# Two layers of a graph transformer on one core: VectorE and GpSimd in program order, a third tile's own query, queries moved ahead in layer 1, weight loads moved to GpSimd

## The chip, the core and the metric

The kernel runs on one core of a Trainium2 chip. A core has engines that run side by side, each with its own stream of instructions: TensorE (PE) multiplies matrices into an accumulation memory (PSUM), VectorE (DVE) and ScalarE (ACT) work elementwise, GpSimd (POOL) does small elementwise work and starts gathers and scatters by index, SyncE (SP) starts transfers. Each engine takes its instructions in the order in which they stand in its stream, and waits at an instruction until what it reads is there and what it overwrites is free. The metric is the device time of one execution in microseconds; the time before is the median of three runs, 1954.13 us (1949.94 to 1956.24).

## What is computed

The reference, cut to what matters. There are 2708 tokens of width 512 and a symmetric adjacency matrix with about eight neighbours a token. Both layers are the same, with their own weights.

```python
def layer(h, adj, Wq, bq, Wk, bk, Wv, bv, Wo, bo, W1, b1, W2, b2, g1, s1, g2, s2):
    n = h.shape[0]                                   # 2708
    mask = adj.astype(float32) + eye(n)
    q = (h @ Wq.T + bq).reshape(n, 8, 64)            # 8 heads of 64
    k = (h @ Wk.T + bk).reshape(n, 8, 64)
    v = (h @ Wv.T + bv).reshape(n, 8, 64)
    scores = einsum('nhd,mhd->hnm', q, k) / sqrt(64)
    scores = where(mask == 0, -1e9, scores)
    ctx = einsum('hnm,mhd->nhd', softmax(scores), v).reshape(n, 512)
    h1 = layer_norm(h + ctx @ Wo.T + bo, g1, s1)
    ff = relu(h1 @ W1.T + b1) @ W2.T + b2            # 512 -> 2048 -> 512
    return layer_norm(h1 + ff, g2, s2)
out = layer(layer(x, adj, *weights0), adj, *weights1)
```

## The kernel before, in words

The tokens make 22 tiles of 128 (the last has 20). Attention is done by edges: a token has at most 22 neighbours, so instead of full scores the kernel makes a list of neighbours for each token, sorts the tokens by the number of their neighbours, and gathers for each slot of a list one row of 1024 numbers (key and value) per token. Tile g of the sorted order has `CAPS[g]` slots, from 22 to 3. A second path, `by_rows`, computes the same without lists; it runs behind a flag that is set where a list does not fit, and it does not run here.

Stages of the first path, `by_edges`:

1. *Keys* (`first`). For each of 22 tiles, TensorE makes k and v from x and the weights Wk, Wv (`project`, eight instructions of 128x512 each). VectorE adds the bias to k (L910), ScalarE copies v (L912), and a transfer writes both to memory. Beside it `lists(t)` reads 128 rows of the adjacency (1.35 MB), adds the diagonal on GpSimd (L683), turns them into codes on ScalarE (L687), and finds the neighbours with MAX8 on VectorE (11 instructions of L690, then three MAX8 and two MATCH_REPLACE). With `LEAD = 1.3` the code writes 1.3 lists a tile. At tile `QT = 6` the bias row bq is made from a column (`turned_row`): four products with the identity on VectorE (`dg`, L559), four matmuls (`pr<-dg`, L565), a copy (L566). Wo and the first two weight pairs W1, W2 are loaded near the end of the stage, by SyncE.
2. *Queries of layer 0* (`first_queries`). TensorE makes the queries of 22 tiles, VectorE scales them (L947), and they go to memory (q_d). In between the lists are ranked and inverted (`ranked`, `inverted`, L843 and L852), which gives `ident_i`, the token in each place of the sorted order. Everything that goes by the sorted order is gathered by GpSimd with it. The first two tiles of the order get their query here from their own gathered rows (`own_rows`, `own_query`), at query `OWN = 6`, so that their attention can begin before all queries are in memory.
3. *Feed-forward of layer 0* with attention beside it. Blocks are pairs of tiles in the order (20, 19), (18, 17), (7, 9), (6, 10), (5, 11), (0, 16), (1, 15), (2, 14), (3, 13), (4, 12), (21, 8). In a block, `feed_forward` runs 16 steps f: four matmul pairs into `pf` (L1428), relu on ScalarE into `ft` (L1439), and three steps later two accumulations into the block's accumulators a0 and a1 (L1401). During the steps of block k the attention of block k + 1 is brought to its end: at step 10 its context `cx` is turned (`tp<-ident,cx`, L1236), at step 11 it is projected with Wo (L578), added to the residual (L1363) and normed (`norm`, L1217 to L1230, with `rd` on GpSimd, L1226); after step 15 the result h is turned for the next block. At a block's end the accumulators are added to h (L1460) and normed. In layer 0 the next layer's keys and values of the block before follow in steps 5 to 8 (`keys_values`). The rows bk and bq for layer 1 are turned in blocks 1 and 3: `dg` at step 1, `pr` at step 3.
4. *Layer 1* the same way, from its own queries: the queries of the first `AHEAD = 8` blocks stand ahead of its feed-forward, those of the others in blocks 0 to 2. At the end `checked` makes the flag, which the engines load before they branch.

Attention is a generator (`attend`) of chunks of two slots. A chunk's `weights` multiplies the gathered keys by the query (L1100) and sums them to scores (L1106); one chunk later `weigh` takes the exponentials on ScalarE (L1119) and weighs the values on ScalarE (L1126) and VectorE (L1132, added up in L1139); two chunks later, at a tile's last chunk, `sums` closes the tile (L1147, L1151, L1159, and the reciprocal L1162); three chunks later `divided` makes `cx` on ScalarE (L1170). Gathers (L1063) are written three chunks ahead of their use. `advance(more)` adds to a credit and runs chunks until it is used up, a chunk of two slots costing one:

```python
        while credit > 0 and len(got) < CXB - 1:
...
                advance(PACE[n] if k else 0.8 if f < 11 else 0.4)
```

so that `PACE` chunks stand beside each step, and at most two finished tiles wait in `got`.

**What sets the order on each engine.** Within `tc.manual_schedule(engines=...)` the named engines keep the order in which the code writes their instructions. Outside it a planner sorts an engine's instructions by its own estimate of when each can run. TensorE, ScalarE and SyncE are in program order throughout (L495). GpSimd is in program order up to the end of layer 0's first block (L1608, closed at L1703). VectorE is in the planner's order for the keys, in program order from the last two key tiles to step 14 of layer 0's first block (L901, L1610, closed at L1650), and in the opening of layer 1 (L1620). Instructions that are written after such a region may still be put between those inside it.

## Time and profile before

| | us |
|---|---|
| median of three runs | 1954.13 |
| the profiled execution | 1960.03 |
| its span, first to last instruction | 1958.1 |
| TensorE busy | 1856.4 |
| VectorE busy | 1328.4 |
| ScalarE busy | 933.0 |
| GpSimd busy | 804.6 |
| mean granted TensorE clock | 0.979 |

The prediction reads four views: the page (busy time of each engine), the waits (who waited for whom), busy time by stretch, and the timeline of an engine (start, duration, engine, line, operation, output<-inputs, count, and in brackets the idle time before it and what ended it). PE is TensorE, DVE VectorE, ACT ScalarE, POOL GpSimd. In the table by stretch the columns are: from:to, length, busy us of PE, its weight loads, DVE, ACT and POOL with numbers of instructions, then the granted TensorE clock, the busy share of the transfer engines, and GB/s. The keys take the first 160 us, the queries of layer 0 go to 261, layer 0's feed-forward to 1118, layer 1's opening to 1212.

### The profile page before, as it was taken

Reading aid. Unit: us, or ns where it says so; the run is one execution under the profiler, and the core shown is the slowest. Engines: PE = TensorE matmul, PEld = TensorE weight load, DVE = VectorE, ACT = ScalarE, POOL = GpSimd, SP = SyncE. Lnnn points to the kernel's source line nnn. Section 1 sums busy time; section 2 is a strip of 40 time slices with the busy share of each in tenths; the row PEclk is TensorE's granted clock in tenths of the full one; section 3 lists DMA queues with packets and bytes.
Section 4 is the critical chain, followed back from the end, with each engine's and each line's share of the span. In section 5 each row is a group of like instructions: output and inputs, shape, how many; then the busy total and the mean of one; then the engine's idle time right before and its main releaser. Section 6 shows DMA issues by size and latency. Waiting matters only on the chain. (4 is left out here: it accounts for less than half of the span.)

```text
span 1958.1 us, 20848 instructions
## 1 busy us (share of the span) xinstructions
PE 1856.4 (95%) x6160; PEld 1094.8 (56%) x6160; DVE 1328.4 (68%) x2181; ACT 933.0 (48%) x3217; POOL 804.6 (41%) x709
## 2 busy tenths in 40 slices
PE   8998987999999999999999997789899999999996
PEld 4443454655656556566566534456566665666663
DVE  5887676686857868668423256666987998878421
ACT  4561344464545655546422123545475766654520
POOL 2111566453544736545211041333554775546100
PEclk9999998999999999999999999899999999999998
DMA  8988956465645746544210785635664766644000
GB/s 314 344 310 286 348 201 232 160 208 174 219 153 183 244 156 220 181 162 132 102 54 33 263 324 173 208 118 176 215 232 162 245 224 218 197 154 133 17 6 14
DMA packets 133659, 366.91 MB, mean 187 GB/s; under 512 B 19290, under 2 KB 39594, under 8 KB 130828
## 3 DMA queue, kind: packets, MB, share of 16 engines
q0 software_dynamic: 69136, 246.88, 37.9%
q1 hardware_dynamic: 52756, 98.61, 14.6%
q10 hardware_dynamic: 11644, 20.00, 2.8%
q8 instruction: 50, 0.82, 0.2%
q14 instruction: 73, 0.60, 0.1%
HBM read 314.79 MB, written 50.65 MB: 187 GB/s over the span
## 5 line engine op out<-in xcount | busy, mean ns | idle before, releaser
L1063 POOL DMA_INDIRECT kv<-kv_d,listed x420 | 546.6, 1301 | 456.6 <-DVE acc L1139 277.2
L1428 PE MATMUL pf<-hT,w 128*128 128x256 f32 (+1 forms) x2816 | 636.1, 373 | 7.4 <-ACT ft L1439 4.4
L1401 PE MATMUL a<-w,ft 128*128 128x512 f32 x1312 | 618.4, 598 | 11.0 <-DVE h L1460 7.4
L1428 PEld LDWEIGHTS pf<-hT,w 128*128 128x128 f32 x2816 | 520.9, 191 | 182.2 <-issue 103.6
L1100 DVE TENSOR_TENSOR kv<-kv,q 128x1024 f32<-128x1024 f32 (+3 forms) x222 | 255.0, 1159 | 196.6 <-DMA kv<-kv_d,listed 157.9
L1439 ACT ACTIVATE ft<-pf,b 128x256 f32<-128x256 f32 (+1 forms) x336 | 153.9, 463 | 454.3 <-PE pf L1428 454.0
L1401 PEld LDWEIGHTS a<-w,ft 128*128 128x128 f32 x1312 | 248.5, 192 | 203.4 <-issue 168.9
L1126 ACT ACTIVATE kv<-kv,p 128x64 f32<-128x64 f32 x1232 | 311.0, 335 | 5.0
L1106 DVE TENSOR_REDUCE sc<-kv 128x16 f32<-128x1024 f32 (+3 forms) x222 | 254.5, 1154 | 2.0
L1139 DVE TENSOR_TENSOR acc<-acc,kv 128x1024 f32<-128x1024 f32 (+2 forms) x178 | 204.3, 1148 | 20.4 <-ACT kv L1126 17.8
L1226 POOL TENSOR_TENSOR rd<-va,mhalf 128x1 f32<-128x1 f32 (+1 forms) x88 | 90.4, 1027 | 294.9 <-DVE va L1224 294.0
L578 PE MATMUL o<-wo,cT 128*128 128x512 f32 x336 | 149.8, 598 | 0.5 <-ACT cT L1241 0.5
L1132 DVE TENSOR_TENSOR kv<-kv,p 128x512 f32<-128x512 f32 (+1 forms) x178 | 121.8, 685 | 35.0 <-ACT p L1119 35.0
L1119 ACT ACTIVATE p<-sc,listed 128x8 f32<-128x8 f32 x420 | 103.0, 294 | 75.2 <-DVE sc L1106 75.2
L1170 ACT ACTIVATE cx<-acc,su 128x64 f32<-128x64 f32 (+1 forms) x352 | 88.5, 333 | 81.0 <-DVE su L1162 59.8
L578 PEld LDWEIGHTS o<-wo,cT 128*128 128x128 f32 x336 | 64.1, 192 | 82.3 <-issue 72.6
L690 DVE MAX8 tops<-code 128x8 f32<-128x247 f32 (+2 forms) x242 | 83.8, 403 | 23.3 <-ACT code L687 23.2
L687 ACT ACTIVATE code<-aj 128x2708 bf16<-128x2708 int32 (+1 forms) x22 | 73.3, 3331 | 52.6 <-POOL aj L683 52.6
L1230 DVE SCALAR_TENSOR_TENSOR h<-h,rd,ln_b 128x512 f32<-128x512 f32 (+1 forms) x88 | 65.7, 748 | 41.3 <-POOL rd L1226 41.3
L1126 ACT ACTIVATE acc<-kv,p 128x64 f32<-128x64 f32 (+1 forms) x352 | 88.8, 334 | 1.4
L1460 DVE TENSOR_TENSOR h<-a,h 128x512 f32<-128x512 f32 (+1 forms) x44 | 29.9, 680 | 83.3 <-PE a L1401 44.5
L1488 ACT COPY kvs<-v 128x512 f32<-128x512 f32 (+1 forms) x22 | 12.9, 585 | 152.2 <-PE v L578 132.6
(168 smaller groups left out, 1578.6 us busy)
## 6 DMA issues: line engine op xcount, KB each, us to landing
aj<-in_adj SPq DMA_DIRECT2D x21, 1354.0 KB, 8.9
kv_d<-kvs ACTq DMA_DIRECT2D x21, 512.0 KB, 6.5
w<-in_W SPq DMA_DIRECT2D x20, 512.0 KB, 7.5
xg<-in_xT SPq DMA_DIRECT2D x19, 512.0 KB, 9.2
kv<-kv_d,listed POOLq DMA_INDIRECT x420, 5.8
w<-in_W ACTq DMA_DIRECT2D x12, 512.0 KB, 7.6
q_d<-qs SPq DMA_DIRECT2D x22, 256.0 KB, 3.7
zT_d<-zT SPq DMA_DIRECT2D x22, 256.0 KB, 4.8
```

Of the source, the lines that this page charges most:

```text
L578: nc.tensor.matmul(o[:r], xs(c), wm[:, c, :], start=(c == 0), stop=(c == NC - 1))
L1063: return nc.gpsimd.indirect_dma_start(out=to, out_offset=None, in_=table[:, :], in_offset=bass.IndirectOffsetOnAxis(ap=s, axis=0), bounds_ ...
L1100: nc.vector.tensor_tensor(kv[:r, :c, :DM], kv[:r, :c, :DM], self.q[:r].unsqueeze(1).to_broadcast([r, c, DM]), ALU.mult,)
L1106: nc.vector.tensor_reduce(self.sc[:r, s0 : s0 + c, :], kv[:r, :c, :DM].rearrange("p s (h d) -> p s h d", d=DK), AX.X, ALU.add,)
L1119: nc.scalar.activation(p[:r, s, :], self.sc[:r, s, :], AF.Exp, bias=minus[:r, g, s : s + 1])
L1126: nc.scalar.activation(to[:, i, hd], kv[:r, i, DM + h * DK : DM + (h + 1) * DK], AF.Copy, scale=p[:r, s0 + i, h : h + 1],)
L1132: nc.vector.tensor_tensor(to[:, 0, :].rearrange("p (h d) -> p h d", d=DK), kv[:r, 0, DM:].rearrange("p (h d) -> p h d", d=DK), p[:r, s0, : ...
L1139: nc.vector.tensor_tensor(self.acc[:r, :c, :], self.acc[:r, :c, :], kv[:r, :c, DM:], ALU.add)
L1226: nc.gpsimd.tensor_tensor(rd[:r], va[:r], mhalf[:r], ALU.pow)
L1401: nc.tensor.matmul(a[:r], fts[f][:, c0 : c0 + r], self.w2[f // 2][:, f % 2, :], start=(f == 0), stop=(f == NFC - 1),)
L1428: nc.tensor.matmul(pf[:, :w], self.w1[f // 2][:, c, f % 2 * P : f % 2 * P + P], hT[:, c, :w], start=(c == 0), stop=(c == NC - 1),)
L1439: nc.scalar.activation(ft[:, :w], pf[:, :w], AF.Relu, bias=self.b1[:, f : f + 1])
```

## The change

All engines named in `by_hand` now include VectorE and GpSimd, so every engine keeps the order of the code from the first instruction to the last; the regions for single stretches are gone. With it parts of the code are moved:

- A third own query: tile `order[2]` gets its rows with the first two, and its query five tiles after theirs; `OWN` is 7. The lists of the other tiles are all fetched during the queries (`LISTS`), none in block 0. The adds of the last key tile (`last_keys`) stand behind the inversion.
- `AHEAD` is 10: in layer 1, 16 queries stand ahead of block 0's context and four behind it; only block 0 still has queries in its steps.
- Three finished tiles may wait in `got`, `PACE` has three values for a block (steps 0 to 2, 3 to 10, 11 to 15), and in layer 0's first block the turn and projection stand at steps 12 and 13.
- Wo, Wq and four pairs W1, W2 of layer 0 are loaded by GpSimd; the fifth pair by ScalarE.
- Small sums of biases (`unsettled`, `settle`) are made at fixed places.
- The check and the load of its flag move from the end into steps 8 and 14 of the last block.

```diff
-AHEAD = 8
+AHEAD = 10
-OWN = 6
-LISTS = (6, 9, 11, 17, 18, 19)
+OWN = 7
+LISTS = (6, 9, 11, 14, 15, 17, 18, 19, 20, 21)
-PACE = (0.62, 0.72)
+PACE = ((0.45, 0.8, 0.55), (0.5, 0.8, 0.7))
...
         mybir.EngineType.SP,
+        mybir.EngineType.DVE,
+        mybir.EngineType.Pool,
     )
     ctx.enter_context(tc.manual_schedule(engines=set(by_hand)))
...
-            nc.sync.dma_start(out=t[:, c : c + k, :], in_=src[:, c : c + k, :])
+            (by or nc.sync).dma_start(out=t[:, c : c + k, :], in_=src[:, c : c + k, :])
...
-            if t == NT - 2:
-                in_turn.enter_context(tc.manual_schedule(engines={mybir.EngineType.DVE}))
...
             if t == QT:
-                wq = wts.tile([P, NC, DM], F32, tag="wq", name="wq")
-                for c in range(NC):
-                    nc.gpsimd.dma_start(out=wq[:, c, :], in_=chunked(w["Wq"])[:, c, :])
+                wq = matrix(w, "Wq", "wq", nc.gpsimd)
                 turning = turned_row(cols[1], "bq", DK**-0.5)
                 bq = next(turning)
                 finish(turning)
-        in_turn.close()
...
                 evicted(0, held, qs)
-                last_keys()
             if t == 3:
                 inverted(parts)
+                last_keys()
...
-                for g in blocks[0]:
+                for g in order[:3]:
                     own[g] = at.tile([P, DM], F32, tag="q", name="q", bufs=QB)
...
-                xrs = [own_rows(g) for g in blocks[0]]
+                xrs = [own_rows(g) for g in order[:3]]
...
+            if t == OWN + 5:
+                own_query(order[2], zTs[2], to[order[2]], bq, wq)
...
-            self.wo = matrix(w, "Wo", "wo")
+            self.wo = matrix(w, "Wo", "wo", nc.gpsimd if self.n == 0 else None)
...
+        def settle(self):
+            for t in self.unsettled:
+                if isinstance(t, tuple):
+                    nc.vector.tensor_tensor(t[0], t[0], t[1], ALU.add)
+                else:
+                    nc.vector.tensor_scalar(t, t, -1.0, None, ALU.mult)
+            self.unsettled = []
...
+    def settled():
+        held = small.tile([P, 1], F32, tag="held", name="held", bufs=1)
+        nc.vector.tensor_reduce(held, flags, AX.X, ALU.min)
+        pr = ps.tile([P, DM], F32, tag="g", name="pr")
+        nc.tensor.matmul(pr[:1, :1], ones[:, :1], held, start=True, stop=True)
+        nc.vector.tensor_scalar(redo, pr[:1, :1], P - 0.5, None, ALU.is_lt)
+        return nc.values_load(redo[0:1, 0:1], min_val=0, max_val=1)
...
-        while credit > 0 and len(got) < CXB - 1:
+        while credit > 0 and len(got) < CXB:
...
-            now.load_w1(t + 2 - NT)
-            now.load_w2(t + 2 - NT)
+            now.load_w1(t + 2 - NT, nc.gpsimd)
+            now.load_w2(t + 2 - NT, nc.gpsimd)
...
-        if t > 4 and t % 2 and len(now.w2) < 5:
-            now.load_w1(len(now.w1), nc.scalar)
-            now.load_w2(len(now.w2), nc.scalar)
+        if t < 2:
+            now.load_w1(t + 2, nc.gpsimd)
+            now.load_w2(t + 2, nc.gpsimd)
+        if t == 6:
+            now.settle()
+            now.load_w1(4, nc.scalar)
+            now.load_w2(4, nc.scalar)
...
-            streamed = now.queries(order[8 : 2 * AHEAD])
+            streamed = now.queries(order[8:16])
             got = {}
             ahead = attend(n, got)
-            with tc.manual_schedule(engines={mybir.EngineType.DVE}):
...
+            for _ in range(2):
+                now.query(*pool.pop(0))
+            next(ahead)
+            next(streamed)
+            while pool:
+                advance(0.55)
+                now.query(*pool.pop(0))
+            for _ in streamed:
+                advance(0.55)
+            through(0)
+            early[n] = now.attended(blocks[0], got)
+            next(early[n])
+            streamed = now.queries(order[16 : 2 * AHEAD])
+            next(streamed)
+            for _ in blocks[0]:
                 next(early[n])
+            finish(streamed)
...
-                if k + n == 0:
-                    for g in order[14 + f : 15 + f]:
-                        list_of(g)
...
-                advance(PACE[n] if k else 0.8 if f < 11 else 0.4)
+                advance(PACE[n][(f > 2) + (f > 10)] if k else 0.8 if f < 11 else 0.4)
...
+                if last and not more and f == 8:
+                    checked()
+                if last and not more and f == 14:
+                    again = settled()
```

## The prediction, made before the changed kernel ran

> **What bounds the kernel now.** The page comes first. TensorE has work for almost the whole span; the engine whose order changes, VectorE, is at 68%.
>
> ```profile
> PE 1856.4 (95%) x6160; PEld 1094.8 (56%) x6160; DVE 1328.4 (68%) x2181; ACT 933.0 (48%) x3217; POOL 804.6 (41%) x709
> ```
>
> The two programs hold the same TensorE work but for one extra query, so all that can be won is TensorE's idle time, 1958.1 - 1856.4 = 101.7 us. The second view is the waits of TensorE (for whom: us in total, times, longest):
>
> ```profile
> PE tp L1236 <- ACT cx L1170: 35.1, 7, 11.8
> PE tp L1236 <- DVE h L1230: 9.8, 7, 2.5
> PE a L1401 <- DVE h L1460: 7.4, 1, 7.4
> ...
> PE tp L1236 <- DMA xr<-in_x,ident_i: 4.6, 2, 4.5
> ```
>
> It waits mostly for attention (cx) and for norms (h), both made on VectorE. The third view, busy time by stretch, says where: after "us," come the length, then the engines' busy us.
>
> ```profile
> 57.00:77.00 20.00, 20.00 (x50) 9.02 (x50) 17.50 (x66) 12.03 (x7) 4.33 (x10) 1.00 1.00 382
> ...
> 262.00:344.00 82.00, 65.82 (x221) 41.74 (x221) 60.58 (x79) 40.09 (x153) 53.27 (x44) 0.92 0.74 252
> 344.00:1118.00 774.00, 760.23 (x2628) 463.03 (x2627) 494.08 (x703) 377.65 (x1397) 320.86 (x257) 1.00 0.50 165
> 1118.00:1212.00 94.00, 79.85 (x202) 34.54 (x200) 59.23 (x90) 22.92 (x89) 32.58 (x30) 0.95 0.64 239
> 1212.00:1298.00 86.00, 74.82 (x244) 46.64 (x245) 57.03 (x75) 43.42 (x166) 27.65 (x24) 0.92 0.58 188
> 1298.00:1386.00 88.00, 75.65 (x240) 44.95 (x239) 60.80 (x83) 45.82 (x177) 35.00 (x32) 0.92 0.53 175
> ```
>
> TensorE idles 16.2 us in block 0 of layer 0, 13.8 in the ten blocks after it, 14.2 in layer 1's opening and 23.5 in its first blocks. VectorE is not full there either: both wait. The fourth view, the order in time around the longest wait, shows why:
>
> ```profile
> 304.59 0.23 DVE L1159 TENSOR_REDUCE su<-p 128x8 f32<-128x56 f32 x1
> 313.37 1.22 DVE L1100 TENSOR_TENSOR kv<-kv,q 128x1024 f32<-128x1024 f32 x1 [8.54 <-DMA kv<-kv_d,listed]
> 314.51 0.20 DVE L1162 RECIPROCAL su<-su 128x8 f32<-128x8 f32 x1
> ...
> 315.38 1.91 PE L1236 MATMUL tp<-ident,cx 128*128 128x128 f32 x4 [11.75 <-ACT cx L1170]
> 317.08 3.44 PE L1428 MATMUL pf<-hT,w 128*128 128x256 f32 x8
> ```
>
> The code writes the reciprocal L1162 directly behind L1159. The planner put a later tile's L1100 between them; its rows had not landed, and a 0.2 us instruction that TensorE needs stood 8.5 us behind it.
>
> **The change, part by part.** The signs are those of the time.
>
> *Layer 0, block 0.* Program order puts L1162 back behind L1159, and the third tile's own query lets its attention run during the queries. The waits of this block, 11.75 before the turn of cx, 3.2 and 1.2 for ft, and the slow restart go. The restart is in the rows: eight pf took 3.44 us where 1.89 is usual, four turns 1.91 for 1.04, so 2.4 us. The Trainium skill ("TensorE: Matmul & The Clock Gate", Part 1) says that an idle window of 3.4 us halves the clock and about 3.4 us of work restore it: 1.7 us a restart. I take the rows, here 2.4; by the rule (five restarts gone, one new, at 1.7) the total below would be -21.6 for -20.4. The rule speaks against this change too, as the next part shows. New here: the fourth tile's query still comes through memory (in before this kind of row landed 5.8 us after the last query), and from there 10.6 chunks stand before the residual add; at 4.1 us a chunk (L1100, L1106, L1132 and L1139: 1.16 + 1.15 + 0.69 + 1.15) the add comes 7 us late, of which the turn of h passes on about 5. Sum: -11.75 - 4.4 - 2.4 + 5 = -13.5.
>
> *The keys, from the start.* VectorE is now in program order here too. The row bq is turned at tile 6: four diagonal products on VectorE (dg), then four matmuls (pr) on TensorE, in front of tile 7's keys. In before the planner made dg at once:
>
> ```profile
> 8.26 0.66 DVE L559 TENSOR_SCALAR dg<-ident,bq 128x128 f32<-128x128 f32 x3
> ...
> 75.54 0.25 DVE L694 MAX8 top<-cb 128x8 f32<-128x88 f32 x1
> ...
> 56.38 1.05 PE L565 MATMUL pr<-dg,ones 128*128 128x128 f32 x8
> ```
>
> In the changed order nine lists stand ahead of dg. The ninth ended at 75.5 (second line), because lists go at the pace of the adjacency loads. TensorE gets to pr at 56.4 and now finds nothing: 75.5 + 0.9 for dg - 56.4 = 20 us. Nothing covers it, since all keys of tiles 7 to 21 stand behind pr, and they were TensorE-bound (20.00 of 20 us busy in 57 to 77). With TensorE still, fewer bytes compete with the adjacency, and a load lands in 6.9 us at best against 8.9 in the median: 18 to 20, and I take 19. After it the clock is low once, +2. What is late next: the lists, behind the copies of tile 7 on ScalarE, by 12 us; but then keys come every 6.9 us and lists every 6.4, and each add still meets its buffer. The old wait of 2.3 at tile 18 goes. Sum: +18.7.
>
> *Queries of layer 0.* The last keys' adds (4.9 us on VectorE) go behind the inversion, and own queries come one tile later: the waits of 4.6 for xr and 1.3 for kvs go, and a third xr may cost 0.5. The third own query costs TensorE 3.4 + 0.5. Wo and four weight pairs move to GpSimd's queue, which idles 28.6 us ahead of the inversion: 12 issues of about 0.6 (the four for Wq took 2.37) cost nothing; without that cover some 7 us of late gathers. Sum: -1.5.
>
> *The other blocks of layer 0.* The 13.8 us go with the order that made them. New: dg for bk and bq (blocks 1 and 3) now stands behind both norms of the block before (3.6 each) and a chunk, at 12.6 and 16 us after the first accumulator is done, where TensorE wants it at 11.2: +1.4 and +5. Late sums at block ends add 3; there is room here, as a block lasts 78 us on TensorE with the next layer's keys and VectorE has 69 (12.8 chunks, norms, adds). Sum: -4.4.
>
> *Layer 1, opening.* Four more queries (13.7 us) fill the waits before block 0's cx; VectorE has no foreign L1100 ahead of its sums. Of 14.2 idle and 3.2 slow, some 7 stay: the first rows of keys cannot come sooner (3.0, and 1.8 slow), and two turns of 1.1. Sum: -10.5.
>
> *Layer 1, blocks.* The waits were 11.2, 12.3 and 3.0, with 3.8 of slow restarts: -30.3. But program order makes VectorE follow TensorE twice a block. Counted in the two orders of instructions (a chunk of one row as 0.6), blocks 1 to 5 now hold 13.2, 13.8, 12.6, 13.0 and 12.6 chunks of attention (before: 10.2, 10.2, 11, 13.6, 10.6), since the pace is higher after step 2 and three finished tiles may wait where two could: 54 us at 4.1, and four norms of 3.6 make 68 against TensorE's 63.7. Block by block: TensorE needs 40.5 us from a block's start to the residual add (12 pf and 9 accumulations of 1.72, a turn of 0.9, o 3.4) and 20.7 from there to the first finished accumulator (o 3.4, four steps of 3.44, a turn, three matmuls of 0.86); VectorE needs 8 to 8.6 chunks, 33 to 35 us, for the first, and two norms with 4.6 to 5.6 chunks, 26 to 30, for the second. The second tile's add L1460 frees its accumulator; the next block wants it after four pf and half an accumulation, 7.75 us. Carried from block to block, it is over that by 0, 7.0, 2.6, 4.2, 2.6 and 1.2 us: +17.6. Block 0 keeps 2. Sum: -10.7.
>
> *End.* The check moves into the last block: TensorE waits once for the flag, 1.5 us (0.47 for the load, the rest for its VectorE steps). The tail stays: last scatter, then a GpSimd drain of 8.6 us. Sum: +1.5.
>
> Total: -13.5 + 18.7 - 1.5 - 4.4 - 10.5 - 10.7 + 1.5 = -20.4. The profiled execution took 1960.0 us (span 1958.1, and 1.9 around it), 5.9 over the median of 1954.1. It would become 1939.6; on the median's scale **1934 us**.
>
> **Rivals.** (1) *The wait at bq is hidden* because lists come sooner, or VectorE catches up in layer 1 so that L1460 is never late: 1934 - 18 = 1916; with both, 1898. For it: the old order, too, ran 1386 to 1577 with no wait at 54 us of VectorE in 64. Against it: the ninth list hangs on a load, not on VectorE. (2) *VectorE in program order becomes the bound in layer 1*: slower. Place: L1100 waits for its rows, or the norm for GpSimd's rd behind gathers, with the rest of the chunk behind it. Each 0.1 us on a chunk is 1.3 us a block, and over seven blocks 9; at 0.25 us a chunk the gain is gone, and at 0.5 the time is 1934 + 44 = 1978. For it: L1100 was idle 158 us in before for rows. Against: those waits came with buffers held by hoisted chunks; in program order a gather is written three chunks, 12 us, ahead, and took 5.8 to land. (3) *The order does nothing for TensorE, gains and the bq wait cancel*: 1954. For it: the sum is a small difference of large terms, 81 us of waits go and 61 come.
>
> **How the numbers follow.** The likeliest case, the sum as it stands, has 0.48 and its own range is 1920 to 1947. Rival 1 has 0.24 (1895 to 1920), rival 2 0.19 (1955 to 1990), rival 3 0.09 (1948 to 1960). Eight in ten lie from 1902 to 1964. The least that this measurement tells from no change is about 0.3%, 6 us: faster 0.74 (the first two and a little of the third), same 0.08, slower 0.18.
>
> **What would show it.** A TensorE gap of 17 to 21 us near 56 us, ended by dg at the second pr, with the low clock behind it; if it is missing, the largest cost is wrong. No wait for cx above 4 us in layer 0's block 0 and in layer 1's blocks 0 to 2; L1162's successor always behind its L1159. In layer 1 waits of 2 to 7 us for L1460's successor at block starts 2 to 5, none after block 7; if every block shows them, or the chunk grows past 4.3 us, rival 2 holds. The prediction is wrong in sign if the waits in layer 1 sum to more than 45 us.

## The result: slower, 2005.0 us for 1953.9

| | before | after |
|---|---|---|
| median of four runs, us | 1953.91 (1949.94 to 1956.24) | 2004.99 (2003.86 to 2005.82) |
| ratio, 95% interval | | 1.0263 (1.0245 to 1.0281) |
| profiled execution, us | 1960.03 | 2005.24 |
| its span, us | 1958.1 | 2003.5 |
| granted clock | 0.979 | 0.975 |

The change made the kernel 2.6% slower. The forecast was 1934 us, with 1902 to 1964 as its range. Busy time on the page of the changed kernel:

```profile
PE 1872.3 (93%) x6172; PEld 1102.0 (55%) x6172; DVE 1388.8 (69%) x2181; ACT 935.0 (47%) x3218; POOL 753.9 (38%) x721
```

No engine has much more work. TensorE's twelve more instructions are the third own query's, 3.4 us at their spacing. VectorE is busy 60 us longer with the same 2181 instructions, of which more at the end. So the time went mostly into waits, and TensorE's list of waits (for whom: us in total, times, longest) has a new head:

```profile
PE pf L1431 <- ACT ft L1442: 42.4, 12, 9.2
PE a L1404 <- ACT ft L1442: 29.2, 15, 4.6
PE pr L567 <- DVE dg L561: 22.2, 3, 17.9
PE pf L1431 <- ACT hT L1239: 7.3, 6, 2.0
PE o L580 <- ACT cT L1239: 5.1, 1, 5.1
```

The wait for cx that led the list before (35.1 us) is gone altogether, as forecast, and so are those for h and for the accumulator's add. In their place TensorE waits 71.6 us for ft, the relu on ScalarE: 9.6 in layer 0's first block, 29.7 in its others, 32.3 in layer 1's blocks. Before, it was 8.0 us:

```profile
PE pf L1428 <- ACT ft L1439: 4.4, 2, 3.2
PE a L1401 <- ACT ft L1439: 3.6, 3, 2.8
```

The prediction has this wait only among those that would go, in block 0 of layer 0; as a new cost it stands nowhere in it.

The table cuts both spans at the first `pf` of each block, in us from start to start of matmuls. Stage 0 is keys and queries, stages 1 to 11 are blocks 0 to 10 of layer 0 (11 with layer 1's opening behind it), stages 12 to 22 blocks 0 to 10 of layer 1. **Where an expectation below names blocks 2 to 9, 13 to 17 or 13 to 20, these are the stages of this table**; the blocks 1 to 9 of one of them are stages 2 to 10. Each span begins 5.1 us ahead of stage 0; the last line takes in the tail behind the last matmul.

| stages | before | after | difference | forecast |
|---|---|---|---|---|
| 0: keys, queries | 256.7 | 270.5 | +13.8 | +17.2 |
| 1: block 0, layer 0 | 83.5 | 75.5 | -8.0 | -13.5 |
| 2 to 10: blocks 1 to 9 | 723.9 | 756.0 | +32.1 | -4.4 |
| 11: block 10 and opening, less 13.8 for four more queries | 143.4 | 141.9 | -1.5 | -10.5 |
| 12 to 20: blocks 0 to 8, layer 1, plus the same 13.8 | 630.3 | 645.4 | +15.1 | -10.7 |
| 21, 22 and tail | 115.2 | 109.0 | -6.2 | +1.5 |
| all | | | +45.3 | -20.4 |

Two terms miss by 36.5 and 25.8 us, and both are blocks of feed-forward.

What happens there is seen in stage 7, around 836 us, in the timelines of the changed kernel (start, duration, engine, line, operation, output<-inputs, count, and the idle time before it with what ended it). TensorE first, from the projection `o`:

```profile
821.78 4.88 PE L580 MATMUL o<-wo,cT 128*128 128x512 f32 x11
826.50 1.89 PE L1431 MATMUL pf<-hT,w 128*128 128x256 f32 x8
...
833.39 1.89 PE L1431 MATMUL pf<-hT,w 128*128 128x256 f32 x8
835.12 1.88 PE L1404 MATMUL a<-w,ft 128*128 128x512 f32 x4
842.06 3.78 PE L1431 MATMUL pf<-hT,w 128*128 128x256 f32 x8 [5.07 <-ACT ft L1442]
845.64 2.38 PE L1404 MATMUL a<-w,ft 128*128 128x512 f32 x4
```

Three pf, one for each of the three buffers, and the fourth must wait until ScalarE has emptied the first. ScalarE and VectorE at the same time:

```profile
824.24 0.49 ACT L1117 ACTIVATE p<-sc,listed 128x8 f32<-128x8 f32 x2 [0.89 <-DVE sc L1104]
824.76 2.02 ACT L1124 ACTIVATE acc<-kv,p 128x64 f32<-128x64 f32 x8
837.20 0.49 ACT L1117 ACTIVATE p<-sc,listed 128x8 f32<-128x8 f32 x2 [10.41 <-DVE sc L1104]
837.72 2.02 ACT L1124 ACTIVATE kv<-kv,p 128x64 f32<-128x64 f32 x8
839.64 2.00 ACT L1168 ACTIVATE cx<-acc,su 128x64 f32<-128x64 f32 x8
841.55 0.81 ACT L1442 ACTIVATE ft<-pf,b 128x256 f32<-128x256 f32 x2
```

```profile
826.05 0.68 DVE L1366 TENSOR_TENSOR h<-o,xb 128x512 f32<-128x512 f32 x1
826.77 0.69 DVE L1369 TENSOR_TENSOR h<-h,bo 128x512 f32<-128x512 f32 x1
...
830.38 0.68 DVE L1366 TENSOR_TENSOR h<-o,xb 128x512 f32<-128x512 f32 x1
...
834.69 1.22 DVE L1098 TENSOR_TENSOR kv<-kv,q 128x1024 f32<-128x1024 f32 x1
835.94 1.22 DVE L1104 TENSOR_REDUCE sc<-kv 128x16 f32<-128x1024 f32 x1
```

ScalarE had nothing to do from 826.8 to 837.2, with a finished pf in front of it from 828.4 on (826.50 + 1.89). It stood at the exponentials `p` of a chunk whose scores VectorE made behind both residual adds and norms (826.05 to 834.69, then 2.5 us for the chunk), and the code had written that `p`, its weighing and the `cx` behind it ahead of the relu. From the first residual add to the relu it is 15.5 us; TensorE's three buffers cover 10.3 from the end of o. The rest is the 5.1 us.

In the kernel before, at the same place, VectorE had made its scores ahead of the residual adds. Behind the one of 807.70 it made none until 829.08, and ScalarE's exponentials in between found theirs ready:

```profile
807.70 1.22 DVE L1106 TENSOR_REDUCE sc<-kv 128x16 f32<-128x1024 f32 x1
...
812.99 0.68 DVE L1363 TENSOR_TENSOR h<-o,xb 128x512 f32<-128x512 f32 x1
813.59 0.68 DVE L1132 TENSOR_TENSOR kv<-kv,p 128x512 f32<-128x512 f32 x1
...
829.08 1.22 DVE L1106 TENSOR_REDUCE sc<-kv 128x16 f32<-128x1024 f32 x1
```

```profile
817.26 0.47 ACT L1439 ACTIVATE ft<-pf,b 128x256 f32<-128x256 f32 x1 [0.21 <-PE pf L1428]
817.63 0.48 ACT L1119 ACTIVATE p<-sc,listed 128x8 f32<-128x8 f32 x2
818.14 2.02 ACT L1126 ACTIVATE acc<-kv,p 128x64 f32<-128x64 f32 x8
```

The chunk that does this is written by one call that the diff does not touch, between and behind the two residual adds of step 11:

```python
                    for hs_next in projecting:
                        advance(0.5 if k else 0.0)
                advance(PACE[n][(f > 2) + (f > 10)] if k else 0.8 if f < 11 else 0.4)
```

A chunk's exponentials are written one chunk later than its scores. One chunk in this step is harmless: it brings the exponentials of the chunk before, whose scores stand ahead of the residual adds. A second chunk in the same step brings the exponentials of the first, and these must wait until VectorE is through both norms. In block 0 of a layer (k = 0) the call writes nothing, and block 0 of layer 1 (stage 12) is the only block there with attention beside it that shows no wait: 68.4 us, all of it matmul time. It also holds less attention than the five blocks behind it (VectorE busy 53.3 us for 65 to 68), so by itself it proves nothing; the experiments do.

### The profile page after: what moved, and what is told of

Read it like the earlier page. It is cut to its first block, busy times and chain, and to the rows that moved or that the text cites. A ratio compares the mean times of both kernels' runs of the same rounds, so it can differ in the third digit from the quotient of the medians.

```text
span 2003.5 us, 20880 instructions
## 1 busy us (share of the span) xinstructions
PE 1872.3 (93%) x6172; PEld 1102.0 (55%) x6172; DVE 1388.8 (69%) x2181; ACT 935.0 (47%) x3218; POOL 753.9 (38%) x721
## 5 line engine op out<-in xcount | busy, mean ns | idle before, releaser
L1431 PE MATMUL pf<-hT,w 128*128 128x256 f32 (+1 forms) x2816 | 645.0, 377 | 50.6 <-ACT ft L1442 42.4
L1404 PE MATMUL a<-w,ft 128*128 128x512 f32 x1312 | 628.4, 605 | 29.2 <-ACT ft L1442 29.2
L1061 POOL DMA_INDIRECT kv<-kv_d,listed x420 | 506.5, 1206 | 234.5 <-issue 107.3
L1224 POOL TENSOR_TENSOR rd<-va,mhalf 128x1 f32<-128x1 f32 (+1 forms) x88 | 81.9, 931 | 638.9 <-DVE va L1222 638.9
L1098 DVE TENSOR_TENSOR kv<-kv,q 128x1024 f32<-128x1024 f32 (+3 forms) x222 | 256.6, 1156 | 19.3 <-DMA q<-q_d,ident_i 12.8
L1117 ACT ACTIVATE p<-sc,listed 128x8 f32<-128x8 f32 x420 | 104.9, 298 | 352.8 <-DVE sc L1104 346.4
L580 PEld LDWEIGHTS o<-wo,cT 128*128 128x128 f32 x336 | 64.5, 193 | 87.5 <-issue 71.6
L1488 DVE TENSOR_TENSOR kvs<-k,bk 128x512 f32<-128x512 f32 (+1 forms) x22 | 15.2, 689 | 130.2 <-PE k L580 128.9
L692 DVE MAX8 tops<-code 128x8 f32<-128x247 f32 (+2 forms) x242 | 78.6, 399 | 22.6 <-ACT code L689 22.4
L1024 POOL DMA_INDIRECT kv_d<-kvs,ident_i x22 | 24.7, 1124 | 166.0 <-ACT kvs L1491 123.6
```

Source lines behind the costliest of these rows:

```text
L580: nc.tensor.matmul(o[:r], xs(c), wm[:, c, :], start=(c == 0), stop=(c == NC - 1))
L1061: return nc.gpsimd.indirect_dma_start(out=to, out_offset=None, in_=table[:, :], in_offset=bass.IndirectOffsetOnAxis(ap=s, axis=0), bounds_ ...
L1098: nc.vector.tensor_tensor(kv[:r, :c, :DM], kv[:r, :c, :DM], self.q[:r].unsqueeze(1).to_broadcast([r, c, DM]), ALU.mult,)
L1117: nc.scalar.activation(p[:r, s, :], self.sc[:r, s, :], AF.Exp, bias=minus[:r, g, s : s + 1])
L1404: nc.tensor.matmul(a[:r], fts[f][:, c0 : c0 + r], self.w2[f // 2][:, f % 2, :], start=(f == 0), stop=(f == NFC - 1),)
L1431: nc.tensor.matmul(pf[:, :w], self.w1[f // 2][:, c, f % 2 * P : f % 2 * P + P], hT[:, c, :w], start=(c == 0), stop=(c == NC - 1),)
```

## The experiments

**Which part of the change costs it?** The change is an order for two engines and a set of moves. First the order without the moves:

```diff
         mybir.EngineType.SP,
+        mybir.EngineType.DVE,
+        mybir.EngineType.Pool,
     )
```

> The kernel before with one edit: VectorE and GpSimd in program order throughout, and nothing else of the change. Theory (the order on VectorE is the loss: the scores come behind norms and residual adds, ScalarE stands at the exponentials, and the relu that TensorE needs stands behind them): 1985 to 2010 us, a wait of 15 to 20 us at the second pr, and waits of TensorE for ft above 40 us in all. Rival (the loss comes from the new pace and the third finished tile, the order by itself is harmless but for bq): 1945 to 1970, ft waits below 15 us.

Measured: 2087.5 us, 1.0693 (1.0671 to 1.0715). Far above both ranges. TensorE waited 98.4 us for ft, and 17.9 at the second pr. With VectorE alone in the list:

```diff
         mybir.EngineType.SP,
+        mybir.EngineType.DVE,
     )
```

> The kernel before with VectorE in program order throughout and GpSimd left to the planner after block 0. If the loss of the order alone (134 us) is VectorE's: 2070 to 2090. If GpSimd's order (gathers and rd in program order) carries much of it: 2000 to 2040.

Measured: 2091.7 us, 1.0702 (1.0677 to 1.0727), with 94.4 us for ft. The two intervals overlap: the loss of the order alone is VectorE's, and GpSimd's order behind block 0 adds nothing that can be measured. And the moves without the order, both engines given back to the planner by the regions that the diff takes out:

```diff
-        mybir.EngineType.DVE,
-        mybir.EngineType.Pool,
...
+                if f == 14:
+                    in_turn.close()
...
+            with tc.manual_schedule(engines={mybir.EngineType.DVE}):
```

> The changed kernel with VectorE and GpSimd given back to the planner in all stretches where the kernel before had them; own query, queries ahead, pace, limit of finished tiles and moved loads stay as changed. With the order alone the time was 2087.5, with order and moves 2005: if the moves are worth the same without the order, this gives some 1870 (impossible, the matmuls alone take 1852); if they only repair what the order breaks: 1945 to 1965; if they are made for program order and harm the planner: 1975 to 2010.

Measured: 2003.7 us, 1.0262 (1.0231 to 1.0293), the third case. So the order alone costs 134 us, the moves alone 49, both together 51: the moves repair most of what the order breaks, and under the planner they are harmful (TensorE waited 55.9 us for norms, 17 times; before 9.8, 7 times). Neither part can be priced without the other. The mixed version, GpSimd in order and VectorE by the planner, with the same regions for it:

```diff
-        mybir.EngineType.DVE,
         mybir.EngineType.Pool,
```

> The changed kernel with VectorE given back to the planner in the stretches where the kernel before had it (keys, layer 0 after block 0, layer 1's blocks); GpSimd stays in program order, and pace, third own query, queries ahead and the moved loads stay. Theory (order on VectorE): no gap at the second pr, ft waits of TensorE below 20 us, 1935 to 1955 us. Rival (pace and third tile are to blame): only the bq gap goes, ft waits stay above 50 us, about 1980 to 1988.

Measured: 2037.6 us, 1.0443 (1.0423 to 1.0464): neither case. The keys did return to 253.0 us (270.5 in the changed kernel), but VectorE now waited 228 us for gathered rows that GpSimd fetched in the code's order, and TensorE's waits went to norms (25.1), ft (42.2), hT (19.2) and accumulators (17.2). The run therefore says nothing on ft by itself.

**Is it the exponentials?** Here p no longer waits for the scores:

```diff
-                    p[:r, s, :], self.sc[:r, s, :], AF.Exp, bias=minus[:r, g, s : s + 1]
+                    p[:r, s, :], ident[:r, :NH], AF.Exp, bias=minus[:r, g, s : s + 1]
```

> The changed kernel, in which the exponentials on ScalarE read eight columns of a constant in place of the scores: the attention weights are left out, the instructions, shapes and their order stay, and only the wait of p for sc is gone. Theory (relu stands behind p, p behind a late sc): TensorE's waits for ft fall from 71.6 to below 10 us and the time to 1935 to 1955. Rival (VectorE is late in any case and TensorE would meet it at the accumulators and turned rows instead): ft waits fall, other waits come, and the time falls by less than 25 us, to 1980 or more.

Measured: 1993.4 us, 1.0211 (1.0191 to 1.0231). The rival's time: my theory in this form failed. Waits for ft were still 51.1 us, and those for hT, which ScalarE makes too, rose from 7.3 to 23.0. ScalarE's own list of waits shows what took the place of p (346.4 us in the changed kernel, 75.2 before):

```profile
ACT cx L1168 <- DVE su L1160: 193.6, 32, 14.4
```

The division `cx` hangs on VectorE too (on `su`), and stands ahead of the same relu. So the next run freed both:

```diff
-                    cx[:r, hd], self.acc[:r, 0, hd], AF.Copy, scale=self.su[:r, h : h + 1]
+                    cx[:r, hd], ident[:r, :DK], AF.Copy, scale=mhalf[:r]
```

> The changed kernel with ScalarE freed from VectorE in the attention: the exponentials read a constant in place of the scores (as in the run before) and the division of cx reads a constant in place of the summed values and the reciprocal. Attention weights and division are left out; instructions, shapes and order stay. With the scores alone freed the waits for ft went from 71.6 to 51.1 us because cx took the place of p in front of the relu. Theory (ScalarE in order behind VectorE is the channel): with both gone the waits for ft fall below 10 us and layer 0's blocks 1 to 9 together come within 15 us of their matmul time of 78 each; total 1940 to 1960. Rival (VectorE itself is late, and TensorE meets it at accumulators and norms): ft waits vanish, waits for a, h and hT take their place, and the time stays above 1975.

Measured: 1964.9 us, 1.0055 (1.0036 to 1.0073), between the two. Its waits of TensorE:

```profile
PE a L1404 <- DVE h L1463: 24.5, 12, 2.5
PE pr L567 <- DVE dg L561: 23.3, 3, 17.1
PE a L1404 <- ACT ft L1442: 8.6, 3, 3.6
PE pf L1431 <- ACT hT L1239: 7.5, 3, 5.4
PE pf L1431 <- ACT ft L1442: 7.2, 1, 7.2
```

Waits for ft fall to 15.8, and stages 2 to 9 from 679.8 to 653.6 us. Stages 13 to 20 hardly gain (563.2 to 555.0): there the accumulator's late add L1463 comes out from behind the relu, 18.2 of its 24.5 us in layer 1's blocks. That is the wait which the prediction had put there. Each reading holds in a part of the kernel.

**The keys.** The largest single gap, 17.9 us at the second pr, should go if dg is written early:

```diff
             if t == 0:
                 finish(turning)
+                turning = turned_row(cols[1], "bq", DK**-0.5)
+                bq = next(turning)
...
-                turning = turned_row(cols[1], "bq", DK**-0.5)
-                bq = next(turning)
                 finish(turning)
```

> The changed kernel with the four diagonal products for bq moved from tile 6 to tile 0 on VectorE, ahead of the lists. If the gap of 18.1 us at the second pr costs its full length and one slow restart: 1985 us (-18 to -22). If the lists or the adjacency then bound the keys stage and take part of it back: 1992 to 1998. Waits for ft stay at about 72 us in both cases.

Measured: 1998.6 us, 1.0233 (1.0206 to 1.0261): 6.4 us of the 20. Directly behind the old gap's place stands the next wait, for the bias add of a key, which follows the same lists on VectorE:

```profile
64.91 5.13 PE L580 MATMUL k<-wk,xg 128*128 128x512 f32 x8 [7.63 <-DVE kvs L911]
```

A second one of 3.5 us comes at tile 18. The bq row was only the first instruction that found VectorE behind its lists.

**Can the order stay, with other places?** One kernel with an edit for each stage; the edit for bq is the one just shown:

```diff
-LEAD = 1.3
+LEAD = 1.05
-PACE = ((0.45, 0.8, 0.55), (0.5, 0.8, 0.7))
+PACE = ((0.45, 1.1, 0.25), (0.45, 0.85, 0.6))
...
                     for hs_next in projecting:
-                        advance(0.5 if k else 0.0)
+                        pass
```

> The changed kernel, VectorE and GpSimd still in program order, with one edit for each stage. Keys: bq's diagonal products at tile 0 and lists written 1.05 for each tile of keys in place of 1.3, so that a key's add stands behind fewer lists: the stage falls from 270.5 to 255 us. Layer 0's blocks: no attention written between the residual adds, pace 1.1 before them and 0.25 behind them: blocks 2 to 9 fall from 680 us to 640 to 655 if VectorE's lateness at the residual is the cause; no change if VectorE's amount of work is. Layer 1's blocks: the same gap, and a lower pace (0.45, 0.85, 0.6; some 11.2 chunks a block for 12.9): blocks 13 to 17 fall from 355 us to 330 to 340. In all 1930 to 1960 us; the rival, that order in itself costs this time wherever the chunks stand, gives 1985 or more.

Measured: 1898.5 us (1894.8 to 1898.8), 0.9717 (0.9696 to 0.9738): 2.8% faster than before, and better than any case that I had written down. Stages 2 to 9 take 631.3, stages 13 to 17 321.4 us; most blocks run at their matmuls' own time, 78.3 and 63.7. The keys missed their 255: 261.5, since fewer lists ahead leave the last ones, and the counting behind them, for the end (9.6 us of waits there). Then each part was put back. The call between the adds:

```diff
                     for hs_next in projecting:
-                        pass
+                        advance(0.5 if k else 0.0)
```

> The retimed kernel (1898.5 us) with one part undone: half a chunk's credit of attention is written again between and behind the two residual adds of each block. If attention between the residual adds is what puts p and cx in front of the relu: layer 0's blocks 2 to 9 rise from 631 us by 12 to 30, waits for ft come back to 25 us or more, layer 1's blocks 13 to 20 rise from 512 by 10 to 25; in all 1920 to 1950. If the pace alone made the difference: within 5 us of 1898.5.

Measured: 1988.9 us, 1.0170 (1.0131 to 1.0208): 90 us for one call, near twice the most that I expected, with 71.8 us of waits for ft. The pace:

```diff
-PACE = ((0.45, 1.1, 0.25), (0.45, 0.85, 0.6))
+PACE = ((0.45, 0.8, 0.55), (0.5, 0.8, 0.7))
```

> The retimed kernel with the changed kernel's pace (0.45, 0.8, 0.55 and 0.5, 0.8, 0.7) put back, the residual adds still without attention between them. If the pace behind the residual adds (0.55 for 0.25 in layer 0) and the amount in layer 1 (11.9 chunks for 11.2) matter as much as the gap: layer 0's blocks 2 to 9 rise from 631 by 8 to 20 and layer 1's 13 to 17 from 321 by 8 to 15; in all 1912 to 1930. If the gap between the adds is all: within 6 us of 1898.5.

Measured: 1905.9 us, 0.9761 (0.9728 to 0.9793): between the cases, nearer the second; stages 2 to 9 rise by 6 us, 13 to 17 not at all. So with the call gone the pace is worth 7 us: it was a bystander. Two further edits, for the two waits that were left in stages 0 and 1:

```diff
-LEAD = 1.05
+LEAD = 1.15
...
-                if more and f == 10 + 2 * (k + n == 0):
+                if more and f == 10 + 3 * (k + n == 0):
...
-                if more and f == 11 + 2 * (k + n == 0):
+                if more and f == 11 + 3 * (k + n == 0):
...
-                advance(PACE[n][(f > 2) + (f > 10)] if k else 0.8 if f < 11 else 0.4)
+                advance(PACE[n][(f > 2) + (f > 10)] if k else 0.0 if n == 0 and f < 3 else 0.8 if f < 11 else 0.4)
```

> The retimed kernel with two more edits, each in its own stage. Keys: 1.15 lists for each tile in place of 1.05, since now the counting behind the last list holds TensorE for 9.6 us at its end: stage 0 falls from 261.5 to 255 to 259. Layer 0's first block: no attention written beside its first three steps and the residual adds one step later, since the relu stands 9.3 us behind exponentials that wait for the fourth tile's query: the block falls from 75.8 to 66 to 71, or stays if the same wait comes at cx instead. In all 1885 to 1893, or 1898 if both only move.

Measured: 1895.5 us (1890.3 to 1896.7), 0.9703 (0.9672 to 0.9734). Stage 0 fell to 251.9 and stage 1 to 71.8 us, but stage 9 rose by 6.7 with a wait of 4.7 for a turned z, whose cause stays open; in time the kernel can't be told from the retimed one (1898.5).

**The one call alone.** In the changed kernel, and nothing else:

```diff
                     for hs_next in projecting:
-                        advance(0.5 if k else 0.0)
+                        pass
```

> The changed kernel with one call taken out: no attention is written between and behind the two residual adds of a block; order, pace, keys and all else as changed. From the retimed kernel with the old pace (1905.9) and the 9 us that the edits in the keys gave there: 1910 to 1920 us. If those 100 us needed the other edits too: above 1950.

Measured: 1913.8 us (1912.7 to 1915.9), 0.9805 (0.9787 to 0.9822). That is inside the forecast: one line turns 2.6% slower into 2.0% faster. The head of TensorE's waits:

```profile
PE pr L567 <- DVE dg L561: 23.0, 3, 18.4
PE pf L1431 <- ACT ft L1442: 9.7, 2, 9.3
```

ScalarE's timeline at the same place in stage 7, where the norm behind the second residual add ends at 818.9:

```profile
807.78 0.48 ACT L1117 ACTIVATE p<-sc,listed 128x8 f32<-128x8 f32 x2
808.29 2.02 ACT L1124 ACTIVATE kv<-kv,p 128x64 f32<-128x64 f32 x8
815.38 0.47 ACT L1442 ACTIVATE ft<-pf,b 128x256 f32<-128x256 f32 x1 [5.08 <-PE pf L1431]
818.83 0.47 ACT L1442 ACTIVATE ft<-pf,b 128x256 f32<-128x256 f32 x1 [2.97 <-PE pf L1431]
821.38 0.49 ACT L1117 ACTIVATE p<-sc,listed 128x8 f32<-128x8 f32 x2 [2.08 <-DVE sc L1104]
```

Now ScalarE waits for TensorE (5.08), as it should, and two relus pass before the exponentials that hang on the norms. ScalarE still waits 226.7 us in all for scores, while TensorE waits 11.1 us in all for ft: a wait of ScalarE costs nothing where no relu is needed behind it.

The same call taken out where the moves are missing, with the order alone and with the planner:

> The kernel before with VectorE and GpSimd in program order, nothing else of the change (2087.5 us), and the same call taken out. If this one call carries most of what the order alone costs: 1960 to 1990 us, with the wait at bq and the even pace of 0.62 and 0.72 behind the residual adds left over. If the order costs it wherever the chunks stand: above 2050.

Measured: 2003.3 us, 1.0264 (1.0246 to 1.0282), from 2087.5: between the two cases. Waits for ft fell from 98.4 to 5.2, but those for cx rose from 20.9 to 42.0.

> The kernel before, VectorE by the planner, with the same call taken out. If the place in the program matters only where VectorE follows it: 1940 to 1965 us. If it matters under the planner too, because ScalarE is in program order in both: below 1930.

Measured: 2052.4 us, 1.0507 (1.0484 to 1.0529): 100 us slower than before, where I expected next to no change. TensorE waits 69.2 us for cx and 45.2 for h. The old pace of 0.62 and 0.72 makes 9.9 and 11.5 chunks a block, and this call adds 1.0. The largest tiles seem to have needed it: stage 5, which prepares the tile of 22 slots, takes 112.7 us for 85.9. That it is the missing amount is argued; no run gives it back to the planner at another place. So the call gives an amount as well as a place, and in the changed kernel the two had to be told apart. Amount kept, place gone, and the reverse, both on the changed kernel:

```diff
-PACE = ((0.45, 0.8, 0.55), (0.5, 0.8, 0.7))
+PACE = ((0.45, 0.925, 0.55), (0.5, 0.925, 0.7))
...
-                        advance(0.5 if k else 0.0)
+                        pass
```

> The changed kernel without attention between the residual adds, and with the credit that this call gave (1.0 chunk a block) put into the eight steps before them: pace 0.925 for 0.8 in both layers, so that a block holds the same nominal 12.4 chunks as the changed kernel. If the place alone costs the 91 us: 1912 to 1925. If the amount costs it: 1985 or more. If each has its layer (place in layer 0, amount in layer 1, where 12.6 chunks and four norms fill VectorE beyond TensorE's 63.5): layer 0's blocks 2 to 9 near 640, layer 1's blocks 13 to 17 back at 340 or more, 1930 to 1950 in all.

```diff
-PACE = ((0.45, 0.8, 0.55), (0.5, 0.8, 0.7))
+PACE = ((0.45, 0.675, 0.55), (0.5, 0.675, 0.7))
```

> The changed kernel with the call kept and the pace of the eight steps before it lowered by the same 1.0 chunk a block (0.675 for 0.8), so that a block holds the nominal 11.4 chunks of the kernel without the call. If the place costs the 91 us: 1985 to 2010. If the amount costs it: 1912 to 1925. If each has its layer: layer 0's blocks 2 to 9 stay above 670, layer 1's 13 to 17 fall below 335, 1960 to 1980.

Measured: 1936.4 us, 0.9910 (0.9891 to 0.9930), and 1985.4 us, 1.0153 (1.0127 to 1.0179). The first is its third case, in the stages too (637.2 and 342.2). The second stands at the edge of its first case, and its stages fit none (667.2 and 345.9).

The nominal chunks are the sum of the paces and the call over the 16 steps of a block; the rows give layer 1's, and layer 0 has 0.9 fewer in each.

| nominal chunks a block, layer 1 | with the call | without | the place |
|---|---|---|---|
| 12.4 | 2005.0 | 1936.4 | 68.6 |
| 11.4 | 1985.4 | 1913.8 | 71.6 |
| the amount | 19.6 | 22.6 | |

By stage, at 12.4 chunks, the place is worth 42.6 us in stages 2 to 9 (679.8 to 637.2), 12.9 in 13 to 17 and 11.9 in 18 to 20. At 11.4 chunks it is 27.8, 25.2 and 18.8 there: the sum holds, its split does not. The amount, without the call, is worth -2.2, 21.5 and 3.3: nothing in layer 0, and nearly all in the five blocks of layer 1 that hold the most chunks; with the call it is 12.6, 9.2 and -3.6. Without the call VectorE is busy for nearly the whole of these five blocks. The second of them (from:to, length, then busy us of PE, its weight loads, DVE, ACT, POOL), first at 12.4 chunks, then at 11.4, both without the call:

```profile
1354.00:1424.60 70.60, 66.08 (x226) 41.71 (x226) 66.78 (x88) 43.05 (x164) 37.38 (x32) 0.98 0.63 223
```

```profile
1353.50:1417.40 63.90, 63.86 (x225) 41.33 (x226) 60.14 (x81) 40.28 (x153) 34.12 (x28) 1.00 0.59 206
```

VectorE is busy 95% and 94% of these, and the shorter block is as long as its matmuls. In the longer one, too, TensorE meets VectorE's lateness by way of ScalarE: it waits 3.83 us for cT, which stands behind a p that waited 3.66 for its scores, and in all five blocks 10.6 us for cT and none for the accumulator.

## Why the prediction was wrong, step by step

**The keys** (forecast +18.7, with the queries +17.2; measured +13.8) came as worked out: nine lists ended at 74.6, and TensorE stood for 17.93 us.

```profile
74.52 0.85 DVE L561 TENSOR_SCALAR dg<-ident,bq 128x128 f32<-128x128 f32 x4
...
74.84 2.07 PE L567 MATMUL pr<-dg,ones 128*128 128x128 f32 x8 [17.93 <-DVE dg L561]
```

"Each add still meets its buffer" held only behind this wait: the changed kernel's list has none for a key's add, but with bq out of the way the adds cost 11.2 us.

**Block 0 of layer 0** (-13.5; -8.0). The cx wait went. The late fourth query was the right source, but not the turn of h paid 5 us for it: the relu did, with 9.25, and a slow restart came behind that wait (eight pf in 3.60 us).

**The other blocks of layer 0** (-4.4; +32.1). This is the step that failed. "Late sums at block ends add 3; there is room here, as a block lasts 78 us on TensorE" compares VectorE's amount with a block's length. VectorE did have room: 67.2 us of 86.0 in stage 7. What counts is who waits for it at a given moment, and I followed only TensorE's own waits for VectorE (norms, accumulators, dg). The path from VectorE over ScalarE's queue to the relu was left out, although ScalarE had been in program order all along and the code shows p and cx between two relus. In its place the runs show 29.7 us of waits for ft in these blocks, for the 3 forecast for late sums, and restarts behind five of the waits there; the place of the call that puts p and cx in front of the relu is worth 42.6 us in stages 2 to 9. For each place where VectorE would be late I asked what TensorE waits for, and never what stands behind the `p` that waits on ScalarE.

**Layer 1's opening** (-10.5; -1.5). The same path: cT stood behind a `p`, and the projection waited 5.1 us for it; a wait of 2.7 for a transfer and one of 0.8 for an evicted query were not foreseen either.

**Layer 1's blocks** (-10.7; +15.1). The old waits went, 16.2 us in stage 12 alone. The term for VectorE's lateness, +17.6 from 12.6 to 13.8 chunks a block, was near in size: with the call gone and the amount kept, stages 13 to 17 stand 23.7 us above five times 63.7. One of its factors was too small: a chunk of two slots takes 4.32 us in program order (median of 100 chunks that stand back to back), not 4.1. The path was wrong. It showed as waits for ft, in the run without the call for cT, and only with ScalarE freed as waits for the accumulator. The place of the chunks added 12.9 in these stages and 11.9 in stages 18 to 20, where I had written "none after block 7" of the accumulator's waits.

```profile
843.24 1.22 DVE L1098 TENSOR_TENSOR kv<-kv,q 128x1024 f32<-128x1024 f32 x1
...
847.56 1.22 DVE L1098 TENSOR_TENSOR kv<-kv,q 128x1024 f32<-128x1024 f32 x1
```

**The end** (+1.5; -6.2). "The tail stays" was wrong: from the last scatter's issue to the end it is 5.4 us for 12.8. GpSimd's drain at the end took 1.87 us for 8.64. It comes with the moves: from the last accumulation to the end it is 16.8 us before, 23.6 with the order alone and 9.8 with the moves alone. The load of the flag no longer stands behind the scatter; whether that shortens the drain, no run shows.

Of the rivals, the second (slower, 1978 at 0.5 us a chunk) had the sign but not the cause: rows were waited for 1.6 us, not 158, and L1098 took 1.21 us for the 1.22 of L1100. Yet its sign, a chunk past 4.3 us, did come, by the spacing and not by any one instruction: by the prediction's own 9 us for each 0.1, the 0.2 us are some 18 us, an estimate. The sign for a forecast wrong in direction, over 45 us of waits in layer 1, came only if its opening is counted: TensorE's gaps above 0.6 us are 34.7 us in the blocks and 48.8 with the opening.

**The restart.** I took 2.4 us a restart from one row and misread it: the 1.04 us that I set against four turns are the time of eight, and four take 0.60 us (at 303.03 in before). The rule of the Trainium skill ("TensorE: Matmul & The Clock Gate", Part 1) gave 1.7 as my estimate, for idle windows of 3.4 us. The changed kernel's rows give both sizes. Behind the 5.07 us at 842.06, eight pf took 3.78 us for 1.89 and four a 2.38 for 1.88: 2.4 us. Behind 3.61 us it was the pf alone, 1.8 us, and behind 2.03 nothing to speak of:

```profile
1744.38 3.64 PE L1431 MATMUL pf<-hT,w 128*128 128x256 f32 x8 [3.61 <-ACT ft L1442]
1747.86 1.88 PE L1404 MATMUL a<-w,ft 128*128 128x512 f32 x4
...
1884.93 1.99 PE L1431 MATMUL pf<-hT,w 128*128 128x256 f32 x8 [2.03 <-ACT ft L1442]
```

The length of one wait does not decide it: in before, one of 2.10 us (at 138.66) brought a slow restart, eight v in 5.40 us for 3.60, and one of 3.23 us (at 273.92) none.

## What to carry to other kernels

When an engine is put in program order, follow every engine that reads from it and is itself in order: what costs is not the instruction that waits but the next one behind it that the bound engine needs. Count, between two such instructions (here two relus), what each waits for, and compare it with the buffers in between (here three pf, 10.3 us); how busy an engine is on average does not show it (in stage 7 VectorE was idle for 18.8 us of 86.0). And where and how much are two settings of one call: test them apart, since here the place cost 70 us and the amount 20, and taken out of the kernel before, the same call made it 100 us slower.

## What was not expected

- The parts do not add up: order alone +134 us, moves alone +49, both +51.
- A wait can hide others behind it: some 20 us at bq gave back 6, since waits of 7.6 and 3.5 us stood behind it, and with p freed, cx took its place on ScalarE (193.6 us, 32 times).
- ScalarE's waits for scores fell only from 346.4 to 226.7 us when the time fell by 91: most of them never cost anything.
- Program order itself makes VectorE busy longer. Its 2181 instructions sum to 1470 us before and 1476 after, but its busy time goes from 1328.4 to 1388.8, since they overlap less: in before an instruction of another chain starts 0.08 us ahead of the end of the one in front (812.99 and 813.59 above), while in the changed kernel the next one, which needs its result, starts 0.04 us behind it (826.05 and 826.77). It is the order and not the moves: 1389.9 us with the order alone, 1332.0 with the moves alone.
- The best kernel here (1895.5 us; 1898.5 before its last two edits) keeps the whole change, VectorE and GpSimd in program order included, and moves only when attention is written beside it. TensorE is busy 97% of the span in the latter.
